# First convolution of an attention-and-convolution kernel: image pairs with 2x4 output tiles in place of single images with row pairs, and a head's last sums divided anew among VectorE and ScalarE

## The chip, the cores and the metric

The kernel runs on one core of one Trainium2 chip. A core has TensorE (PE, matrix products into PSUM), VectorE (DVE), ScalarE (ACT), GpSimd (POOL), SyncE (SP, which only issues transfers here) and 16 DMA engines. The metric is the device time of one execution in microseconds; lower is better.

## What is computed

The input x has 16 images of 128 channels by 32 by 32 points. Layer 0 is self-attention with 4 heads of 128 channels over the 1024 points of an image, plus x. Layer 1 is two quantized 3x3 convolutions, each followed by a batch normalisation over all images, and again the layer's input is added.

```python
def layer0(x, w_qkv, b_qkv, w_out, b_out):        # einsums of 1x1 convolutions
    qkv = einsum('bchw,oc->bohw', x, w_qkv) + b_qkv
    ...
    attn = softmax(einsum('bnc,bcm->bnm', q, k) * c ** -0.5)
    out = einsum('bnm,bmc->bnc', attn, v)
    ...
    return einsum('bchw,oc->bohw', out, w_out) + b_out + x

def layer1(x, w1, w2, gamma1, beta1, gamma2, beta2):
    out = act_quant(x)                            # clip to 0..1, 15 levels
    out = batchnorm(conv3x3(out, weight_quant(w1)), gamma1, beta1)
    out = act_quant(out)
    out = batchnorm(conv3x3(out, weight_quant(w2)), gamma2, beta2)
    return out + x
```

The first normalisation needs the statistics of all 16 images of the first convolution, so the second convolution can begin only when the attention of the last image is done.

## The kernel before

Everything concerned lies in `fast_path`. Its first part goes over 64 heads (16 images of 4). A head has 4 steps, and there are 252 steps for all heads but the last, which has a loop of its own in smaller units. In a step `scores` (L543 on) makes four 128x512 tiles of scores on PE (`pss`), ScalarE turns each into exponentials (L551), and VectorE forms their sums and differences for a seven-product scheme: L554, then L555 over two tiles at once, then L558; from a head's second step on L562 or L564 also adds to the running softmax sums `es`. The exponentials of a step are in one of two buffers `e`. `attend` then makes the seven products of the step before (`psa`), the second of which needs what L558 writes. So PE's order is: scores of step s, attention of step s-1, scores of step s+1. Each product of 128 output channels is issued as two halves of 64 columns of the PE array (`halves`, L410 on; the profile shows all products made through helpers as line L403).

Other work is hung on this sequence by a table: `at(step, half, fn, ...)` puts a function behind the scores (half 0) or behind the attention (half 1) of a step, and `run` calls what stands there. All table times are written by hand. Each engine's order is fixed when the program is built; it follows these calls, but not exactly (in the trace a piece of `transform_rows` stands between L555 and L558).

At a head's end (`end` is the first step of the next head) `sum_up` reduces `es` to quadrants (L625) in (end, 0). `evacuate` and three parts of `combine` take the four `psa` banks to SBUF with ScalarE and add them on VectorE, at end, end+1 and end+2. `normalise` at (end+2, 1) calls `inverse_sums`, which moves four 32x32 blocks to the first partitions (L652), sums them, takes the reciprocal (L654 to L658), copies it to the other three quadrants (L660) and spreads it (L664), all on VectorE; then it multiplies and adds to the image's accumulator (L673 to L679).

After an image's fourth head its first convolution is made while the next image's attention runs. `quantize` at (end+3, 0) writes a bf16 image with a border into one of three `pads`. `transform_rows` (L782, at (end+4, 0)) forms four row combinations of 16x34 elements, a scheme that gives two output rows at a time. `rows_product` (at end+6 to end+8) makes four products of three taps each, in halves: 24 matmuls of 512 columns per image into the one PSUM buffer of `ps_m` (`psw`), each copied out by ScalarE (L798). `rows_output` (L805, L806, L808) forms the rows on VectorE, and `first_statistics` takes the normalisation's statistics. `ps_m` is shared with the projections `psu` (steps 1 and 2 of a head) and `psv` (eight half steps of an image's third and fourth head). Images 9 to 14 (`AWAY`) send their convolution result to HBM (`y1d`); the second part reads it back in one transfer (L987). The last image has its convolution after the last head.

Of the kernel before, what the change touches and what calls it, by code (L numbers as in the profile page):

```python
# [9 lines left out]
F32 = mybir.dt.float32  # L10
# [4 lines left out]
PSUM = bass.MemoryType.PSUM  # L15

NH = 4
A_LEVELS = 15.0
W_LEVELS = 7.0
BN_EPS = 1e-5  # L20
# [171 lines left out]
def fast_path(  # L192
# [44 lines left out]
    for n in range(2):  # L237
        nc.gpsimd.memset(late[n][:, 0:1], float((B - 1) * N))

    AWAY = range(9, B - 1)  # L240
    ys = [None if b in AWAY else keep.tile([P, N], F32, name=f"y{b}") for b in range(B)]
    pads = []
    for i in range(NPAD):
        t = padp.tile([P, H + 2, W + 2], BF16, name=f"pad{i}")
# [128 lines left out]
    with ExitStack() as ph:  # L373
# [257 lines left out]
            )  # L631
            return part

        def sum_up(g):
            sides[g] = quadrant_sums(sides[g].rearrange("p a n -> p (a n)"))

        def inverse_sums(g, part, cut):

            n = (cut.stop - cut.start) // Q
            rinv = sums[:, g, cut.start // Q : cut.stop // Q]  # L640
            if g == LAST:

                ps = ps_m.tile([P, n], F32, tag="mm", name=f"psr_{g}_{cut.start}")
                w = part.shape[1] // n
                for i in range(w):
                    product(ps, quad, part[:, ts(i, n)], start=(i == 0), stop=(i == w - 1))
                nc.vector.reciprocal(rinv, ps)
            else:

                side = smp.tile([Q, P // Q, n], F32, tag="side", name=f"side_{g}")  # L650
                for a in range(P // Q):
                    nc.vector.tensor_copy(side[:, a, :], part[ts(a, Q), :])  # L652
                total = smp.tile([Q, n], F32, tag="total", name=f"total_{g}")
                nc.vector.tensor_reduce(total, side.rearrange("p a k -> p k a"), AX.X, ALU.add)  # L654

                first, second = total[:, 0 : n // 2], total[:, n // 2 :]
                nc.vector.tensor_tensor(first, first, second, ALU.add)
                nc.vector.reciprocal(rinv[0:Q, :], total)  # L658
                for a in range(1, P // Q):
                    nc.vector.tensor_copy(rinv[ts(a, Q), :], rinv[0:Q, :])  # L660


            rb = rbp.tile([P, N], F32, tag="rb", name=f"rb_{g}")[:, cut]
            nc.vector.transpose(rb, rinv.unsqueeze(2).to_broadcast([P, n, Q]))  # L664
            return rb

        def normalise(g):
            b, h = heads[g]
            rb = inverse_sums(g, sides.pop(g), slice(0, N))
            av = avs.pop(g)  # L670
            if h == 0:
                accs[b] = accp.tile([P, N], F32, tag="acc", name=f"acc_{b}")
                nc.vector.tensor_tensor(accs[b], av, rb, ALU.mult)  # L673
                return
            nc.vector.tensor_tensor(av, av, rb, ALU.mult)  # L675
            nc.vector.tensor_tensor(accs[b], accs[b], av, ALU.add)
            if h == NH - 1 or g == LAST - 1:

                nc.vector.scalar_tensor_tensor(accs[b], accs[b], bo2_sb, xt[b], ALU.add, ALU.add)  # L679
            if h == NH - 1:  # L680
                nc.sync.dma_start(out=x1d[b], in_=accs[b])
# [25 lines left out]
        def attend_unit(u):  # L707
# [30 lines left out]
            if final:  # L738
                avs[LAST, i] = psa[LAST, i]
                sides[LAST, i] = quadrant_sums(total)  # L740
            elif u + 1 == FIRST_UNIT[i + 1]:
                if i == 0:
                    avs["last"] = stp.tile([P, N], F32, tag="y", name=f"y_{LAST}")
                avs[LAST, i] = avs["last"][:, slice(*GROUPS[i])]
                nc.scalar.copy(avs[LAST, i], psa[LAST, i])
                sides[LAST, i] = quadrant_sums(total)

        def normalise_group(i):
            b, h = heads[LAST]
            x1 = accs[b]  # L750
            cut = slice(*GROUPS[i])
            rb = inverse_sums(LAST, sides.pop((LAST, i)), cut)
            nc.vector.tensor_tensor(rb, avs.pop((LAST, i)), rb, ALU.mult)
            nc.vector.tensor_tensor(x1[:, cut], x1[:, cut], rb, ALU.add)
            done = quantize(b, x1, A_LEVELS, 0.0, cut.start // W, cut.stop // W)
            quantized[:] = [done.ins]
            if i == len(GROUPS) - 1:
                nc.sync.dma_start(out=x1d[b], in_=x1)
# [1 line left out]

        middle1 = once.tile([P, 2, 3, P], BF16, name="middle1")
        taps1 = wq[0].rearrange("p (y x) o -> p y x o", x=3)
        weights1 = (taps1[:, 0], middle1[:, 0], middle1[:, 1], taps1[:, 2])
        D = H // 2
        FOUR = ((0, 2, ALU.subtract), (1, 2, ALU.add), (2, 1, ALU.subtract), (1, 3, ALU.subtract))
        works, ms = {}, {}

        def transform_weights():  # L770
            with tc.issue_after(sums_added[0]):
                nc.vector.tensor_tensor(middle1[:, 1], taps1[:, 0], taps1[:, 2], ALU.add)
                nc.vector.tensor_tensor(middle1[:, 0], middle1[:, 1], taps1[:, 1], ALU.add)
                nc.vector.tensor_tensor(middle1[:, 1], middle1[:, 1], taps1[:, 1], ALU.subtract)

        def transform_rows(b):
            pad = pads[b % NPAD]
            works[b] = once.tile([P, 4, D, W + 2], BF16, tag="rows", name=f"rows_{b}")
            pick = lambda r: pad[:, r : r + 2 * D - 1 : 2, :]
            for k in (1, 2, 0, 3):  # L780
                x_, y_, op = FOUR[k]
                nc.vector.tensor_tensor(works[b][:, k], pick(x_), pick(y_), op)  # L782

        def rows_product(b, k):
            ps = ps_m.tile([P, D, W], F32, tag="mm", name=f"psw_{b}_{k}")
            for dx in range(3):
                halves(
                    ps,
                    lambda t: weights1[k][:, dx, LANES[t]],
                    works[b][:, k, :, dx : dx + W],  # L790
                    start=(dx == 0),
                    stop=(dx == 2),
                )
            inner = k in (1, 2)
            if k < 2:
                ms[b, inner] = qtp.tile([P, 2, D, W], F32, tag="qt", name=f"m_{b}_{k}")

            nc.scalar.mul(ms[b, inner][:, k // 2], ps, (1.0, 0.5, 0.5, -1.0)[k])  # L798

        def rows_output(b):  # L800
            inner, others = ms.pop((b, True)), ms.pop((b, False))
            if b in AWAY:
                ys[b] = stp.tile([P, N], F32, tag="y", name=f"y_{b}")
            both = once.tile([P, 2, D, W], F32, tag="tiles", name=f"both_{b}")
            nc.vector.tensor_tensor(both[:, 0], inner[:, 0], inner[:, 1], ALU.add)  # L805
            nc.vector.tensor_tensor(both[:, 1], inner[:, 0], inner[:, 1], ALU.subtract)  # L806
            y = ys[b].rearrange("p (i r w) -> p r i w", r=2, w=W)
            nc.vector.tensor_tensor(y, others, both, ALU.add)  # L808

        def first_statistics(b):  # L810
            statistics(b, 0)
            if b in AWAY:
                nc.sync.dma_start(out=y1d[b - AWAY.start], in_=ys[b])

        def first_conv(r, rows, group):

# [53 lines left out]
        for g in range(LAST):  # L870
            b, h = heads[g]

            end = (g + 1) * NK
            at(end, 0, sum_up, g)
            at(end, 1, evacuate, g)
            at(end + 1, 0, combine, g, 0)
            at(end + 1, 1, combine, g, 1)
            at(end + 2, 0, combine, g, 2)
            at(end + 2, 1, normalise, g)
            if g > 0:  # L880
                at(g * NK + 1, 0, project_u, g + 1, 0)
                at(g * NK + 2, 0, project_u, g + 1, 1)
            if h == NH - 1:
                at(end + 3, 0, lambda b: quantize(b, accs[b], A_LEVELS, 0.0), b)
                at(end + 3, 1, sums_range, b)
                at(end + 4, 0, transform_rows, b)
                for i, k in enumerate((1, 2, 0, 3)):
                    at(end + 6 + (i + 1) // 2, (i + 1) % 2, rows_product, b, k)
                at(end + 8, 1, rows_output, b)
                at(end + 9, 0, first_statistics, b)  # L890
                if b + 2 < B:
                    at(end + 5, 0, load, b + 2, nc.scalar)
            elif h == NH - 2 and b + 1 < B:

                when = ((4, 0), (4, 1), (6, 1), (7, 0), (7, 1), (8, 0), (8, 1), (9, 1))
                for i, (step, half) in enumerate(when):
                    at(g * NK + step, half, project_v, b + 1, *divmod(i, 2))
        at(2, 1, project_u, 1, 0)
        at(3, 1, project_u, 1, 1)
        at(n_steps, 1, gather, 0)  # L900

        for step in range(n_steps):
            g, k = divmod(step, NK)
# [289 lines left out]
def attention_then_quantized_convs(  # L1193
# [49 lines left out]
    def conv_weights(n, wp, behind):  # L1243
# [15 lines left out]
            wq[n].rearrange("p t o -> p (t o)"), raw, MAGIC, None, ALU.subtract  # L1259
        )  # L1260

        nc.vector.tensor_scalar(sc[n], alpha, 1.0 / (A_LEVELS * W_LEVELS), None, ALU.mult)

    flag = const.tile([1, 1], mybir.dt.int32, name="flag")
    fast_path(
# [84 lines left out]
```

## Time and profile before

| | |
|---|---|
| median of two runs | 2024.57 us (2023.04 to 2026.1) |
| the profiled execution, its own time | 2024.57 us |
| its span, first to last instruction | 2022.7 us |
| PE, DVE, ACT busy | 1987.6, 1722.2, 1198.5 us |
| first part, steps of heads | to about 1894 us |
| from there to the end | last head, second convolution, output |

Busy times are unions of the records of an engine. A record of VectorE usually ends a little after the next one has begun, so a group's sum of durations is larger than the time it occupies. PE's ends are modelled, and two halves of the array can be at work at once, so PE's rows are read by the starts of their instructions. In steady stretches two images take 238.8 us, always the same.

### The profile page before, as it was taken

Reading aid. Unit: us, or ns where it says so; the run is one execution under the profiler, and the core shown is the slowest. Engines: PE = TensorE matmul, PEld = TensorE weight load, DVE = VectorE, ACT = ScalarE, POOL = GpSimd, SP = SyncE. Lnnn points to the kernel's source line nnn. Section 1 sums busy time; section 2 is a strip of 40 time slices with the busy share of each in tenths; the row PEclk is TensorE's granted clock in tenths of the full one; section 3 lists DMA queues with packets and bytes.
Section 4 is the critical chain, followed back from the end, with each engine's and each line's share of the span. In section 5 each row is a group of like instructions: output and inputs, shape, how many; then the busy total and the mean of one; then the engine's idle time right before and its main releaser. Section 6 shows DMA issues by size and latency. Waiting matters only on the chain. (4 is left out here: it accounts for less than half of the span.)

```text
span 2022.7 us, 24701 instructions
## 1 busy us (share of the span) xinstructions
PE 1987.6 (98%) x9497; PEld 730.3 (36%) x9497; DVE 1722.2 (85%) x2642; ACT 1198.5 (59%) x2007; POOL 19.7 (1%) x29
## 2 busy tenths in 40 slices
PE   9999999999999999999999999999999999999994
PEld 3543333333333333333333333433333333333441
DVE  5889888888888888888888888888888888878888
ACT  4565665665566566566556556656656655655575
POOL 0000000000000000000000000000000000000020
PEclk9999999999999999999999999999999999999997
DMA  1000000000000000000000000000000000000064
GB/s 42 24 1 22 1 22 1 22 0 1 22 1 22 1 9 14 0 22 1 21 1 1 22 1 21 11 22 11 1 22 11 22 11 21 11 1 11 11 239 168
DMA packets 12846, 43.74 MB, mean 22 GB/s; under 512 B 1456, under 2 KB 1840, under 8 KB 12720
## 3 DMA queue, kind: packets, MB, share of 16 engines
q1 hardware_dynamic: 9520, 32.05, 4.2%
q10 hardware_dynamic: 3200, 10.03, 1.5%
q8 instruction: 76, 1.25, 0.3%
q14 instruction: 50, 0.41, 0.1%
HBM read 22.16 MB, written 19.92 MB: 21 GB/s over the span
## 5 line engine op out<-in xcount | busy, mean ns | idle before, releaser
L403 PE MATMUL pss<-u,x 128*64 128x512 f32 (+1 forms) x4128 | 1031.9, 589 | 1.6 <-ACT u L509 1.6
L403 PE MATMUL psa<-e,vo 128*64 128x512 f32 (+1 forms) x3624 | 922.4, 588 | 0.0
L551 ACT ACTIVATE e<-pss 128x512 f32<-128x512 f32 x1008 | 595.4, 596 | 380.7 <-PE pss L403 331.9
L403 PEld LDWEIGHTS pss<-u,x 128*64 128x64 f32 x4128 | 351.6, 137 | 549.3 <-issue 493.4
L403 PEld LDWEIGHTS psa<-e,vo 128*64 128x64 f32 x3624 | 304.8, 137 | 483.5 <-issue 449.6
L555 DVE TENSOR_TENSOR e<-e 128x1024 f32<-128x1024 f32 x252 | 307.7, 1221 | 29.8 <-ACT e L551 21.6
L554 DVE TENSOR_TENSOR e<-e 128x512 f32<-128x512 f32 x252 | 172.2, 683 | 105.5 <-ACT e L551 101.7
L558 DVE TENSOR_TENSOR e<-e 128x512 f32<-128x512 f32 x252 | 174.0, 690 | 21.5 <-DVE e L555 0.5
L595 ACT COPY ev<-psa 128x512 f32<-128x512 f32 x252 | 135.5, 589 | 87.2 <-PE psa L403 87.0
L403 PE MATMUL psu<-x,at_sb 128*64 128x512 f32 x512 | 184.9, 599 | 1.0 <-DMA x<-in_x_dram 1.0
L403 PE MATMUL psv<-bt_sb,x 128*64 128x512 f32 x512 | 184.9, 592 | 1.0 <-ACT bt_sb L480 1.0
L530 ACT COPY vo<-psv 128x512 f32<-128x512 f32 x128 | 75.5, 590 | 142.3 <-PE psv L403 142.3
L564 DVE TENSOR_TENSOR es<-es,e 128x1024 f32<-128x1024 f32 x126 | 154.0, 1222 | 2.7
L509 ACT ACTIVATE u<-psu,au_sb 128x512 f32<-128x512 f32 x127 | 87.4, 688 | 21.7 <-PE psu L403 20.1
L798 ACT ACTIVATE m<-psw 128x512 f32<-128x512 f32 x60 | 35.9, 598 | 92.6 <-PE psw L403 90.7
L608 DVE TENSOR_TENSOR y<-ev,y 128x512 f32<-128x512 f32 x63 | 43.6, 692 | 52.4 <-ACT y L606 52.4
L664 DVE STREAM_TRANSPOSE rb<-sums 128x1024 f32<-128x1024 f32 (+1 forms) x66 | 79.8, 1210 | 1.6
L625 DVE TRANSPOSE_TENSOR_REDUCE part<-es 128x32 f32<-128x1024 f32 (+1 forms) x65 | 79.6, 1224 | 1.1
L403 PEld LDWEIGHTS psv<-bt_sb,x 128*64 128x64 f32 x512 | 53.6, 137 | 73.5 <-issue 66.7
L403 PEld LDWEIGHTS psu<-x,at_sb 128*64 128x64 f32 x512 | 53.5, 138 | 73.1 <-issue 69.1
L562 DVE TENSOR_TENSOR es<-e,e 128x1024 f32<-128x1024 f32 x63 | 76.8, 1219 | 0.0
L675 DVE TENSOR_TENSOR av<-av,rb 128x1024 f32<-128x1024 f32 x47 | 57.6, 1225 | 1.6
(159 smaller groups left out, 1193.6 us busy)
## 6 DMA issues: line engine op xcount, KB each, us to landing
x_dram<-acc SPq DMA_DIRECT2D x16, 512.0 KB, 4.3
x<-in_x_dram ACTq DMA_DIRECT2D x15, 512.0 KB, 4.6
res<-x_dram SPq DMA_DIRECT2D x1, 7680.0 KB, 30.0
y_dram<-y SPq DMA_DIRECT2D x6, 512.0 KB, 2.6
back<-y_dram SPq DMA_DIRECT2D x1, 3072.0 KB, 11.4
out_dram<-back SPq DMA_DIRECT2D x6, 512.0 KB, 4.5
out_dram<-y SPq DMA_DIRECT2D x5, 512.0 KB, 4.1
out_dram<-y SPq DMA_DIRECT2D x9, 256.0 KB, 2.5
```

The costliest lines, as they stand in the source:

```text
L403: done = nc.tensor.matmul(out_, lhsT=lhsT, rhs=rhs, start=start, stop=stop)
L509: copied = nc.scalar.activation(dst, ps, AF.Identity, bias=au_sb[:, h : h + 1])
L530: nc.scalar.copy(v[:, c : c + 3 : 2], ps.rearrange("p (h a o) -> p a h o", a=2, o=PH))
L551: exps[:] = [nc.scalar.activation(e[:, 2 * c + 1 - m], ps, AF.Exp).ins]
L554: nc.vector.tensor_tensor(e[:, T3], e[:, B12], e[:, B22], ALU.add)
L555: nc.vector.tensor_tensor(e[:, T1 : T2 + 1 : T2 - T1], e[:, B12 : B11 + 1], e[:, B11 : T3 + 1 : T3 - B11], ALU.subtract)
L558: nc.vector.tensor_tensor(e[:, T4], e[:, T2], e[:, B21], ALU.add)
L562: nc.vector.tensor_tensor(sides[g], es[g, 0][:, T4 : T3 + 1], mine, ALU.add)
L564: added = nc.vector.tensor_tensor(sides[g], sides[g], mine, ALU.add)
L595: nc.scalar.copy(to, ps)
L625: nc.vector.tensor_reduce(part, total.rearrange("p (k c) -> p k c", c=Q), AX.X, ALU.add, apply_transpose=True,)
L664: nc.vector.transpose(rb, rinv.unsqueeze(2).to_broadcast([P, n, Q]))
```

## The change

1. Images are taken in pairs (0 and 1, up to 12 and 13). Along columns four outputs are formed from six input combinations, along rows two outputs from four: 24 products of 256 columns for two images, each in halves, so 48 matmuls of 256 columns per pair, where there were 48 of 512.
2. VectorE forms the combinations: `six_columns` in three stages s = 0, 1, 2 (28 operations of 34x8 elements per pair, which read every fourth bf16 column of `pads`), `six_rows` (24 operations of 2x16x8 elements), and, when ScalarE has copied four products out, the sums in `six_products` (three operations of 512, 256 and 256 elements for each of six columns, and ten of 512 elements per pair that read or write every fourth f32 column of the result `y2`).
3. Image 14 stands alone, with four outputs from 16 products of 256 columns (`transform_columns`, `products`).
4. The weights' transform is larger (some 18 operations, once). The weights and the scale get a factor 24 that cancels.
5. A head's seven 32x32 copies go to ScalarE, `inverse_sums` is cut into `sum_up` parts 1 to 3, and a head's end takes a step more: `combine` parts 1 and 2 at end+2 and end+3, `normalise` at (end+3, 1); quantizing follows at (end+5, 0). The last head of the step loop keeps a shorter plan.
6. Images 6 to 13 send their result away, two per transfer of 1 MB; `y1d` holds eight.

The diff, cut to its core:

```diff
-    AWAY = range(9, B - 1)
+    AWAY = range(6, B - 2)
...
+            elif part == 1:
                 side = smp.tile([Q, P // Q, n], F32, tag="side", name=f"side_{g}")
                 for a in range(P // Q):
-                    nc.vector.tensor_copy(side[:, a, :], part[ts(a, Q), :])
+                    nc.scalar.copy(side[:, a, :], sides[g][ts(a, Q), :])
...
                 for a in range(1, P // Q):
-                    nc.vector.tensor_copy(rinv[ts(a, Q), :], rinv[0:Q, :])
+                    nc.scalar.copy(rinv[ts(a, Q), :], rinv[0:Q, :])
...
+        def six_columns(p, s, g):
+            if g == 0:
+                works[p] = once.tile([P, 8, ROWS, D4], BF16, tag="rows", name=f"work_{p}_{s}")
+            pad = pads[(2 * p + g) % NPAD]
+            at = lambda c: pad[:, :, c : c + 4 * D4 - 3 : 4]
+            one, two = works[p][:, g], works[p][:, 2 + g]
+            t, u = works[p][:, 4 + g], works[p][:, 6 + g]
+            if s == 0:
+                nc.vector.tensor_tensor(t, at(1), at(2), add)
+                nc.vector.tensor_tensor(u, at(3), at(4), add)
+                nc.vector.scalar_tensor_tensor(one, t, -4.0, u, mult, add)
...
+        def six_rows(p, s, i):
+            if i == 0:
+                tiles[p] = once.tile(
                    [P, 2, 4, 2 * D * D4], BF16, tag="tiles", name=f"tiles_{p}_{s}"
                )
+            pick = lambda r: works[p][:, 2 * i : 2 * i + 2, r : r + 2 * D - 1 : 2, :]
+            for k, (x, y, op) in enumerate(OF_FOUR):
+                into = tiles[p][:, i, k].rearrange("p (g i j) -> p g i j", g=2, j=D4)
+                nc.vector.tensor_tensor(into, pick(x), pick(y), op)
...
+        def two_products(name, weights, operands, scale, k):
+            if k == 0:
+                ms[name] = qtp.tile([P, 4, 2 * P], F32, tag="qt", name=f"wino_{name}")
+            ps = ps_m.tile([P, 2, 2 * P], F32, tag="mm", name=f"psw_{name}_{k}")
+            for i in range(2):
+                halves(ps[:, i], lambda t: weights[:, k + i, LANES[t]], operands(k + i))
+            nc.scalar.mul(ms[name][:, k : k + 2], ps, scale)
+            return ms[name]
...
+            nc.vector.tensor_tensor(e, two, of(2).unsqueeze(1).to_broadcast(list(two.shape)), ALU.add)
+            nc.vector.tensor_tensor(e[:, 0], e[:, 0], of(3), ALU.add)
+            nc.vector.tensor_tensor(e[:, 1], e[:, 1], of(3), ALU.subtract)
...
+            elif i == 1:
+                sums, differences = (y[0], y[1]) if s == 0 else (y[2], y[3])
+                nc.vector.tensor_tensor(sums, one, other, ALU.add)
+                nc.vector.tensor_tensor(differences, one, other, ALU.subtract)
+                if s == 1:
+                    nc.vector.tensor_tensor(y[0], y[0], y[2], ALU.add)
+                    nc.vector.scalar_tensor_tensor(y[2], y[2], 3.0, y[0], ALU.mult, ALU.add)
+                    nc.vector.scalar_tensor_tensor(y[1], y[3], 2.0, y[1], ALU.mult, ALU.add)
+                    nc.vector.scalar_tensor_tensor(y[3], y[3], 6.0, y[1], ALU.mult, ALU.add)
...
-            at(end + 1, 1, combine, g, 1)
-            at(end + 2, 0, combine, g, 2)
-            at(end + 2, 1, normalise, g)
+            at(end + 1, int(g < LAST - 1), sum_up, g, 1)
+
+            if g < LAST - 1:
+                at(end + 2, 0, combine, g, 1)
+                at(end + 2, 0, sum_up, g, 2)
+                at(end + 3, 0, combine, g, 2)
+                at(end + 3, 0, sum_up, g, 3)
+                at(end + 3, 1, normalise, g)
...
+                elif b % 2 == 1:
+                    p = b // 2
+                    columns = ((5, 1), (6, 0)), ((8, 0), (8, 1)), ((12, 0), (12, 1))
+                    rows_ = ((6, 1), (7, 0)), ((10, 0), (10, 1)), ((19, 0), (19, 1))
+                    when = ((7, 1), (8, 0), (8, 1), (9, 1)), ((11, 0), (11, 1), (13, 1), (18, 1))
+                    when += (((20, 1), (21, 1), (22, 1), (23, 0)),)
...
+                    at(end + 24, 0, first_statistics, b)
```

## The prediction

> **What bounds the kernel now.** I read the page's busy line and slices first.
>
> ```profile
> PE 1987.6 (98%) x9497; PEld 730.3 (36%) x9497; DVE 1722.2 (85%) x2642; ACT 1198.5 (59%) x2007; POOL 19.7 (1%) x29
> ...
> PE   9999999999999999999999999999999999999994
> ...
> DVE  5889888888888888888888888888888888878888
> ```
>
> PE is full to the last slice. The table of windows shows it head by head, for the four heads of one image (the next image repeats them):
>
> ```profile
> 735.00:765.00 30.00, 30.00 (x142) 10.17 (x140) 26.19 (x42) 18.56 (x31) 0.00 (x0) 1.00 0.10 36
> 765.00:794.50 29.50, 29.50 (x148) 11.06 (x146) 25.02 (x36) 17.65 (x30) 0.00 (x0) 1.00 0.00 1
> 794.50:822.60 28.10, 28.10 (x136) 9.99 (x134) 25.32 (x37) 16.46 (x28) 0.00 (x0) 1.00 0.00 1
> 822.60:854.40 31.80, 31.80 (x150) 10.80 (x148) 26.03 (x42) 18.57 (x33) 0.00 (x0) 1.00 0.00 1
> ...
> sum 238.80, PE 238.80 PEld 84.06 DVE 205.11 ACT 142.48 POOL 0.00; mean PE 29.85 PEld 10.51 DVE 25.64 ACT 17.81 POOL 0.00
> ```
>
> After each length stand PE, PEld, DVE and ACT. PE never stops: the steady part is PE's, and each microsecond taken from PE there is one of time, as long as VectorE keeps up. It has 33.7 us left in 238.8. How late it may be, the timeline shows at the step that starts at 765.05:
>
> ```profile
> 772.50 0.69 DVE L558 TENSOR_TENSOR e<-e 128x512 f32<-128x512 f32 x1
> ...
> 774.25 3.17 PE L403 MATMUL psa<-e,vo 128*64 128x512 f32 x13
> ...
> 777.68 1.22 DVE L562 TENSOR_TENSOR es<-e,e 128x1024 f32<-128x1024 f32 x1
> ...
> 778.99 1.20 ACT L551 ACTIVATE e<-pss 128x512 f32<-128x512 f32 x2 [0.58 <-DVE es L562]
> ```
>
> L558 ends at 773.19, 5.0 us after the step's last exponential (768.18), and its attention starts at 774.25: 1.1 us to spare. In the next step it ends at 776.60, 0.9 us after the last exponential, for an attention at 781.54: 4.9 us. So VectorE may fall some 5 us behind, and the old kernel uses 4 of them after an image's end. A second limit: exponentials of a head's third step wait for L562, since `e` has two buffers (46.9 us of such waits in all, hidden so far by three score banks).
>
> The groups give the sizes:
>
> ```profile
> L403 PE MATMUL psw<-rows,wq 128*64 128x512 bf16 x180 | 37.8, 383 | 0.0
> L403 PE MATMUL psw<-rows,middle 128*64 128x512 bf16 x180 | 37.4, 383 | 0.0
> L282 PE MATMUL psc<-pad,wq 128*128 128x256 bf16 x45 | 5.5, 274 | 0.3 <-DVE pad L1007 0.3
> ...
> L652 DVE COPY side<-part 32x32 f32<-32x32 f32 x252 | 42.9, 170 | 4.6
> L660 DVE COPY sums<-sums 32x32 f32<-32x32 f32 x189 | 32.6, 173 | 3.8
> L782 DVE TENSOR_TENSOR rows<-pad 128x544 bf16<-128x544 bf16 x60 | 24.9, 436 | 0.5
> L654 DVE TENSOR_REDUCE total<-side 32x32 f32<-32x128 f32 x63 | 23.0, 366 | 2.2
> ```
>
> The psw rows overstate PE's cost. In the timeline six of them begin at 1023.30 and regular scores go on at 1024.38; two halves for 1.08 us, less 0.43 each for a psa and a pss within, leave 1.30, so 0.216 us of one half for each: both halves work at once, and 24 cost 24 x 0.108 = 2.6 us per image.
>
> **What the Trainium skill says.** "VectorE: DVE Perf Modes", perf-mode tier table and the errata section: f32 tensor_tensor takes (N+151)/0.96 ns, bf16 goes double only at step 1. The trace agrees: 691 ns for 512 f32 (685 here), (272+151)/0.96 = 441 for the 544 bf16 of L782 (436). "TensorE: Matmul & The Clock Gate", back-to-back issue gap: N/2.4 + 2.5, so 109 ns for 256 columns; the trace has 5.5/45 = 122 at full width. "ScalarE: Activation LUTs", What ACT_TABLE_LOAD costs: 186 + 0.833 N, 93 of it overlapped; 612 for 512 columns, trace 617. "SBUF — State Buffer", Door 1, the note on cachelines: each access to a new 16-byte line pays; f32 at step 4 is just that. No size is given; L654, 128 elements at a wide step, takes 366 where the range's reductions of 128 in a row (L348, L349) take 245 and 278, so up to 0.9 ns an element.
>
> **PE, part by part.** Removed per pair: 48 x 0.108 = 5.2 us. Added: 48 products of 256, per half 24 x 0.109 to 0.122 = 2.6 to 2.9. Saved 2.5 us per pair, 17.3 for seven. Weight loads are 110 ns for bf16 beside 107 of columns; if they don't hide, all is lost, if they do, nothing more comes. Image 14: 2.6 - 16 x 0.11 = 0.8. Sum -18.1.
>
> **VectorE.** An independent successor starts some 0.08 us before a record ends (544 bf16 occupy 0.35 us, 512 f32 0.60, 1024 f32 1.14, by the starts in the timeline). Removed per pair: 56 small copies, 8 x (0.72 + 0.55) = 10.2; row transforms 8 x 0.35 = 2.8; outputs 2 x (0.60 + 0.60 + 1.14) = 4.7: 17.7. Added: six_columns 28 x (0.44 - 0.08) = 10.1; six_rows, 256 elements at double rate, 24 x (0.29 - 0.08) = 5.0, at single rate 8.2; the sums of a column 6 x (0.60 + 2 x 0.34) = 7.7; ten operations on y2 6.0; chained ones wait for each other, 0 to 3, I take 1.5; strided f32 0 to 10 x 512 x 0.9 ns = 4.6, I take 2, since half are writes. Together 32.3, bounds 28.8 and 39.6. Net +14.6 (11 to 22): 219.7 of PE's 236.3 us. It fits on average, not by place. By heads from the pair's end on, VectorE | PE:
>
> head 1 23.3 | 30.0; head 2 29.9 | 27.8; head 3 30.1 | 28.6; head 4 27.6 | 32.0; head 5 29.9 | 30.2; head 6 27.7 | 28.4; head 7 22.9 | 27.5; head 8 24.7 | 31.8.
>
> These are the windows above less 1.3 for the copies, with quantizing (1.7) moved on one head, the old image work out, and the stages where the table puts them: head 2 has s = 0 (twelve column operations 4.3, eight row ones 1.7), head 3 three sums of a column, two of y2, s = 1 and its rows (9.6), head 5 the large output at step 18 and eight row operations at step 19 (6.6). The 3.5 us for chains and strides come on top, mostly in heads 3 and 5.
>
> Heads 2 and 3 ask 60.0 + 1.4 of 56.4 us: 5 us behind, and on top of that the wave within a head (combine and normalise, 4.6 us, now all in its fourth step beside 6.4 us of PE), of which the old kernel's 1.1 us of margin shows the size. Of 5 to 6 us that may be late, 2 to 3 are missing. In head 5, step 18 asks 3.9 for L554 to L564, 1.5 for combine and the sum's chain, 1.3 and 3.6 for sums and result, step 19 asks 3.9, 1.2 for combine, 3.4 + 1.2 for normalise after a fourth head, 1.7 for rows: 22, and 2 for chains and strides, beside PE's 14; the lag starts near zero: again 2 to 3 missing. What is late then is L558 for the attention, and L562, which holds the exponentials of a third step. I take 5 us of new PE stall per pair; bounds 0 (the fixed order puts sums first and the wave doesn't add) and 11.5 (all added work at the upper price).
>
> **The rest.** ScalarE gets 56 x 0.12 to 0.21 us and four more copies of products (2.4): 142.5 becomes about 154 of 236, costs nothing while no copy waits; a copy that waits for a late VectorE sum has exponentials queued behind it, but each now stands a step after its source. ps_m's products are a half step (3 us) from any other use and need 0.6 to be copied. Transfers of y1d: one of 1 MB for two of 512 KB on SP, 17 steps before the buffer is needed: nothing. The read back grows from 3 MB in 11.4 us to 4 MB, about 15.2: issued at 1928.3, there at 1943.5; image 7, now the first in it, is quantized at 1943.7: 0 to 1, I take 0.5. Weights' transform: some 5 us more VectorE once, at 87 busy in 100: 0 to 5, I take 1. Image 14: about 15 us for 4 on VectorE in the last eight steps: 0 to 4, I take 1.
>
> **Sum.** -18.1 + 0.5 + 1 + 1 = -15.6, stalls 7 x 5 = +35: +19.4. Span 2022.7 + 19.4 = 2042.1; 1.9 us lie around it (the execution's own 2024.57 is also the median): 2044.
>
> **Rivals.** (a) The lag is hidden: PE's gain stays, 2009. For it: 16 us still free per pair, order by readiness; against: 60 of 56 in heads 2 and 3. Chance 0.24. (b) Slower by over 2%, VectorE as the bound, by one mechanism: short rows and strides cost more than the plain price. Rows of eight at single rate (3.2) and y2 at the full stride (2.6) give 5.8 us more per pair, in the full heads: 2044 + 7 x 5.8 = 2085. It decides from 8 us of stall per pair, 3 more than I take. For it the L654 row, against it that L782's rows of 34 run double. Chance 0.25. (c) 256 columns don't cost less, weight loads bind: +17 on PE, 3 us less stall per pair: about 2040. Against it 122 ns above, with weights twice as wide. Chance 0.05. My forecast, 2025 to 2065: 0.46.
>
> **How the numbers follow.** 2% is about what a measurement of this kernel can tell from no change: 1984 and 2065. Faster by that would need 40 us, more than PE's 18: 0.02. Slower 0.25, same 0.73. The range goes from (a) with small change, 2007, to (b), 2088; the likeliest's own is 2025 to 2065.
>
> **What would show it.** The psw products: 24 per half at 0.11 us. Steady pairs of 238.8 less 2.5 plus stall; PE below full in head 3 and in steps 18 to 20 after a pair; PE loads waiting for L558's like, ACT for L562's. VectorE near 220 per pair. Wrong if PE stays full (a), if six_columns or y2 rows are far over 0.44 and 0.69 us (b), or if stalls stand elsewhere.

## The result, and the profile after

The changed kernel takes 2095.18 us (two runs, 2093.64 to 2096.73) where the one before takes 2024.57: a ratio of 1.0349, 95% interval 1.0302 to 1.0396. It is slower, by 70.6 us; the prediction said 2044, at most 2088. The span of its profiled execution is 2094.9 us, against 2022.7. Its line numbers are five higher for the attention (scores' exponentials L556, sums L559, L560, L563, running sum L567 or L569), and the products that L403 showed stand in L408.

The page's busy line and slices of PE and VectorE:

```profile
PE 2014.9 (96%) x9505; PEld 890.8 (43%) x9505; DVE 1796.4 (86%) x2692; ACT 1278.9 (61%) x2480; POOL 19.6 (1%) x29
...
PE   8999999999999999999999999999999999999994
...
DVE  4878788897988988898888988989789888889998
```

The slices hide it: PE still shows nine tenths, but a tenth of 52 us is five. The table of windows, one pair cut at the starts of its heads (after each length PE, PEld, DVE and ACT; later the granted clock), shows where PE stands still:

```profile
787.51:818.65 31.14, 29.52 (x139) 13.69 (x135) 27.14 (x44) 18.19 (x39) 0.00 (x0) 1.00 0.00 1
...
910.05:944.07 34.02, 30.76 (x145) 11.57 (x143) 31.29 (x47) 20.04 (x39) 0.00 (x0) 0.95 0.00 1
...
sum 247.24, PE 241.87 PEld 106.54 DVE 215.25 ACT 152.57 POOL 0.00; mean PE 30.23 PEld 13.32 DVE 26.91 ACT 19.07 POOL 0.00
```

A pair takes 247.0 to 247.7 us where it took 238.8. Cut at the starts of PE's scores, six steady pairs are 52 us longer together, the first pair 4, the last 28 steps 15, the part after them 1: the 72 us of the span. Within a pair it is heads 2 and 6, counted from the pair's end, that are longest over their old length, and there PE has gaps of 1.6 and 3.3 us.

The groups, kept apart by form, with the lines that the prediction priced:

```profile
L408 PE MATMUL psw<-tiles,wino 128*64 128x256 bf16 x368 | 64.2, 274 | 0.0
...
L649 ACT COPY side<-part 32x32 f32<-32x32 f32 x252 | 54.5, 216 | 179.1 <-DVE part L630 176.6
L853 DVE TENSOR_TENSOR tiles<-work 128x256 bf16<-128x256 bf16 x168 | 43.6, 283 | 0.0
...
L899 DVE TENSOR_TENSOR y<-six 128x512 f32<-128x512 f32 x14 | 16.1, 1151 | 0.0
L895 DVE TENSOR_TENSOR y<-y,six 128x512 f32<-128x512 f32 x14 | 15.8, 1129 | 0.0
...
L901 DVE TENSOR_TENSOR y<-y 128x512 f32<-128x512 f32 x7 | 7.8, 1120 | 0.0
```

The 274 ns of the psw row are not PE's price, since neighbours overlap. The starts in the timeline are:

```profile
901.86 0.27 PE L408 MATMUL psw<-tiles,wino 128*64 128x256 bf16 x1
...
901.97 0.27 PE L408 MATMUL psw<-tiles,wino 128*64 128x256 bf16 x1
...
902.08 0.59 PE L408 MATMUL pss<-u,x 128*64 128x512 f32 x1
...
902.29 0.38 PE L408 MATMUL psw<-tiles,wino 128*64 128x256 bf16 x2
...
902.51 3.17 PE L408 MATMUL pss<-u,x 128*64 128x512 f32 x14
```

Two products hold one half of the array from 901.86 to 902.08, two the other half from 902.29 to 902.51: 0.11 us each, as predicted.

Two things stand out. The sums that write `y2` take 1.12 to 1.15 us, where 512 f32 in a row take 0.69. And the small copies `side`, which were moved to ScalarE, wait 176.6 us there for VectorE's `part`. One such wait in the timeline, at the start of head 2 (a step's four exponentials are L556; in brackets the idle time before and what ended it):

```profile
787.51 0.60 ACT L556 ACTIVATE e<-pss 128x512 f32<-128x512 f32 x1 [3.31 <-PE pss L408]
...
788.80 1.25 DVE L630 TRANSPOSE_TENSOR_REDUCE part<-es 128x32 f32<-128x1024 f32 x1
...
790.08 0.90 ACT L649 COPY side<-part 32x32 f32<-32x32 f32 x4 [1.97 <-DVE part L630]
790.89 1.54 ACT L556 ACTIVATE e<-pss 128x512 f32<-128x512 f32 x3
...
793.90 0.67 ACT L662 COPY sums<-sums 32x32 f32<-32x32 f32 x3 [1.48 <-DVE sums L659]
...
796.51 0.64 ACT L556 ACTIVATE e<-pss 128x512 f32<-128x512 f32 x1
...
797.21 1.08 PE L408 MATMUL pss<-u,x 128*64 128x512 f32 x4 [1.62 <-ACT e L556]
```

In the table of steps the `side` copies are due in the second half of step end+1. In ScalarE's queue they stand in step end itself, here between its first and its second exponential, in other heads ahead of the first or behind a later one. VectorE, late with its column operations, delivers `part` at 790.05; until then ScalarE is idle for 1.97 us with three exponentials behind it, whose scores PE completes one after the other up to 790.0 (its sixteen score matmuls run from 785.98). The `sums` copies, due in step end+3, stand as early as step end+1 and hold ScalarE for another 1.48 us; the next step's first exponential begins only at 796.51, and PE waits 1.62 us for it.

The second place is head 6, after the six results of a pair (L898 to L904, 906.40 to 912.46):

```profile
914.51 0.69 DVE L563 TENSOR_TENSOR e<-e 128x512 f32<-128x512 f32 x1
...
915.25 4.73 PE L408 MATMUL psa<-e,vo 128*64 128x512 f32 x13 [2.71 <-DVE e L563]
...
918.53 0.90 ACT L649 COPY side<-part 32x32 f32<-32x32 f32 x4 [5.35 <-DVE part L630]
```

Here PE itself waits 2.71 us for L563, which VectorE reaches late behind the six results, and ScalarE stands idle at the copies for 5.35 us. The 13 matmuls after the gap take 4.73 us where 13 take 3.17 elsewhere (before, at 774.25). The windows over it, and those over the same place of a later pair, show why:

```profile
911.51:914.92 3.41, 1.03 (x5) 0.14 (x1) 3.41 (x6) 1.19 (x2) 0.00 (x0) 1.00 0.00 0
914.92:918.34 3.42, 3.09 (x8) 1.00 (x10) 3.42 (x6) 0.00 (x0) 0.00 (x0) 0.50 0.00 0
...
1652.21:1655.62 3.41, 2.52 (x11) 0.59 (x7) 3.41 (x6) 2.39 (x4) 0.00 (x0) 1.00 0.00 0
1655.62:1659.03 3.41, 1.60 (x8) 0.63 (x10) 3.41 (x7) 0.00 (x0) 0.00 (x0) 1.00 0.00 0
1659.03:1662.45 3.42, 3.42 (x22) 1.43 (x19) 3.42 (x5) 1.71 (x6) 0.00 (x0) 1.00 0.00 0
```

The granted clock is 0.50 from 914.92 on, for 3.4 us. "TensorE: Matmul & The Clock Gate" of the Trainium skill, Part 1, tells of such half clock, after an idle window of about 3.4 us. Here less was enough, and the length of the gap alone does not decide: the six steady pairs all have a gap of 2.7 to 3.0 us at this place, five have half clock after it, and the one of the last three lines has not (its gap is 2.70 us).

The half-clock stretches of one run stand on a grid of 3.413 us: the first six of this kernel start 73, 72, 73, 72 and 145 such units apart. Laid on that grid, the windows at full clock of all traces of this case, between 100 and 1900 us, show a rule. After each of the 27 in which PE (by its modelled ends) stood still for 1.94 us or more, the next window is at half clock; it is after none of the 134 with 0.9 to 1.91 us. The gap of 2.70 us lies across a border of the grid and counts as 0.9 and 1.8.

The pair with that gap takes 247.0 us, the five others 247.2 to 247.7. So half clock adds some 0.2 to 0.7 us to a pair, less than the 1.6 us by which it stretches the 13 products, and the rest of the stall is there without it.

### The profile page after: what moved, and what is told of

The parts are those of the page before. It is cut to its first block, busy times and chain, and to the rows that moved or that the text cites. A ratio compares the mean times of both kernels' runs of the same rounds, so it can differ in the third digit from the quotient of the medians.

```text
span 2094.9 us, 25194 instructions
## 1 busy us (share of the span) xinstructions
PE 2014.9 (96%) x9505; PEld 890.8 (43%) x9505; DVE 1796.4 (86%) x2692; ACT 1278.9 (61%) x2480; POOL 19.6 (1%) x29
## 4 chain that ended last, share of the span: by engine, by line
PE 64%; DVE 24%; ACT 8%; issue 3%; DMA 0%; POOL 0%; DVEq 0%; ACTq 0%
PE pss L408 27%; PE psa L408 26%; DVE e L560 4%; PE psv L408 4%; PE psu L408 4%; ACT e L556 3%; DVE es L569 2%; DVE e L563 2%; ACT ev L600 2%; DVE part L630 2%; DVE e L559 1%; DVE es L567 1%; PE psc L287 1%; ACT side L649 1%; DVE av L690 1%
## 5 line engine op out<-in xcount | busy, mean ns | idle before, releaser
L408 PE MATMUL pss<-u,x 128*64 128x512 f32 (+1 forms) x4128 | 1061.0, 592 | 25.8 <-ACT e L556 23.2
L408 PE MATMUL psa<-e,vo 128*64 128x512 f32 (+1 forms) x3624 | 934.6, 595 | 19.3 <-DVE e L563 19.3
L556 ACT ACTIVATE e<-pss 128x512 f32<-128x512 f32 x1008 | 579.9, 594 | 308.3 <-PE pss L408 258.6
L408 PEld LDWEIGHTS pss<-u,x 128*64 128x64 f32 x4128 | 405.5, 137 | 500.6 <-issue 343.1
L408 PEld LDWEIGHTS psa<-e,vo 128*64 128x64 f32 x3624 | 363.4, 138 | 463.7 <-issue 375.0
L560 DVE TENSOR_TENSOR e<-e 128x1024 f32<-128x1024 f32 x252 | 307.2, 1219 | 26.3 <-ACT e L556 23.7
L559 DVE TENSOR_TENSOR e<-e 128x512 f32<-128x512 f32 x252 | 172.2, 683 | 86.0 <-ACT e L556 85.3
L563 DVE TENSOR_TENSOR e<-e 128x512 f32<-128x512 f32 x252 | 172.4, 684 | 10.1 <-DVE e L560 0.9
L408 PE MATMUL psv<-bt_sb,x 128*64 128x512 f32 x512 | 179.7, 593 | 1.0 <-ACT bt_sb L485 1.0
L408 PE MATMUL psu<-x,at_sb 128*64 128x512 f32 x512 | 174.7, 604 | 2.3 <-ACT wino L862 1.5
L649 ACT COPY side<-part 32x32 f32<-32x32 f32 x252 | 54.5, 216 | 179.1 <-DVE part L630 176.6
L569 DVE TENSOR_TENSOR es<-es,e 128x1024 f32<-128x1024 f32 x126 | 153.8, 1220 | 1.9
L862 ACT ACTIVATE wino<-psw 128x512 f32<-128x512 f32 x92 | 55.0, 598 | 70.5 <-PE psw L408 69.3
L679 DVE STREAM_TRANSPOSE rb<-sums 128x1024 f32<-128x1024 f32 (+1 forms) x66 | 79.6, 1207 | 12.0 <-ACT sums L662 11.9
L613 DVE TENSOR_TENSOR y<-ev,y 128x512 f32<-128x512 f32 x63 | 43.3, 688 | 52.8 <-ACT y L611 52.8
L408 PEld LDWEIGHTS psv<-bt_sb,x 128*64 128x64 f32 x512 | 58.7, 137 | 61.3 <-issue 49.2
L408 PEld LDWEIGHTS psu<-x,at_sb 128*64 128x64 f32 x512 | 54.4, 139 | 65.8 <-issue 52.4
L567 DVE TENSOR_TENSOR es<-e,e 128x1024 f32<-128x1024 f32 x63 | 76.8, 1219 | 0.3
## 6 DMA issues: line engine op xcount, KB each, us to landing
back<-y_dram SPq DMA_DIRECT2D x1, 4096.0 KB, 14.1
```

The lines of the kernel that those rows point to most:

```text
L408: done = nc.tensor.matmul(out_, lhsT=lhsT, rhs=rhs, start=start, stop=stop)
L556: exps[:] = [nc.scalar.activation(e[:, 2 * c + 1 - m], ps, AF.Exp).ins]
L559: nc.vector.tensor_tensor(e[:, T3], e[:, B12], e[:, B22], ALU.add)
L560: nc.vector.tensor_tensor(e[:, T1 : T2 + 1 : T2 - T1], e[:, B12 : B11 + 1], e[:, B11 : T3 + 1 : T3 - B11], ALU.subtract)
L563: nc.vector.tensor_tensor(e[:, T4], e[:, T2], e[:, B21], ALU.add)
L567: nc.vector.tensor_tensor(sides[g], es[g, 0][:, T4 : T3 + 1], mine, ALU.add)
```

## The experiments

Two theories were on the table after this. **Q**: the order of ScalarE's queue loses the time, since copies that VectorE feeds stand ahead of exponentials. **V**: VectorE's load loses it, by place, the slow sums on `y2` above all, and the queue only shows it. All times below are medians, read against the kernel before on the same chip (2023.8 to 2025.2 us); losses and gains are differences from it.

**1. Undo the small copies' move.** The changed kernel, with the seven copies of a head back on VectorE.

```diff
-                    nc.scalar.copy(side[:, a, :], sides[g][ts(a, Q), :])
+                    nc.vector.tensor_copy(side[:, a, :], sides[g][ts(a, Q), :])
...
-                    nc.scalar.copy(rinv[ts(a, Q), :], rinv[0:Q, :])
+                    nc.vector.tensor_copy(rinv[ts(a, Q), :], rinv[0:Q, :])
```

> The changed kernel with the seven 32x32 copies of a head on VectorE again, all else kept. Theory Q (ScalarE's queue: the side copies stand ahead of a head's first exponentials and wait for VectorE's part): the stalls at steps 4 and 12 after a pair and part of those at step 20 go, some 6 us per pair, so about 2050 us. Theory V (VectorE has too much work, the strided result above all): VectorE gets 10 us more per pair, so slower than the changed kernel's 2095, 2110 or more.

Measured: 2099.8 us (2097.85 to 2100.28), ratio 1.0366 (1.0349 to 1.0383). Q's 2050 is missed by far, and so is V's 2110: the 4 us over the changed kernel lie within the two intervals. The waits only moved: two copies in `combine`, which were on ScalarE before the change too and read VectorE's sums (L617 and L620), now hold the exponentials.

```profile
ACT ev L620 <- DVE y L618: 57.9, 39, 2.2
...
ACT ev L617 <- DVE y L613: 24.8, 24, 1.6
```

**2. Take the stride out of the results.** The changed kernel, with the four outputs of a row as four planes of `y2` instead of every fourth column. What is left out: the second convolution doesn't put the planes together again and reads points at wrong places.

```diff
-                y2[p].rearrange("p g (i j c) -> p (g i) j c", j=D4, c=4)[..., c] for c in range(4)
+                y2[p][:, :, ts(c, N // 4)] for c in range(4)
```

> The changed kernel with the pair's result kept in four planes of 256 elements in a row, so that the ten operations on it have no step of 16 bytes. The points of an image then lie in another order, and the second convolution reads them at wrong places. Both theories: these operations take 0.69 us and not 1.12. Q: only the stall at step 20 shrinks, 2 to 3 us per pair, so 2070 to 2080. V: most stalls go, 2020 to 2035.

Measured: 2071.8 us, ratio 1.0228 (1.0211 to 1.0246). The sums fall to the plain price:

```profile
L898 DVE TENSOR_TENSOR y<-six 128x512 f32<-128x512 f32 x14 | 9.5, 682 | 0.0
...
L901 DVE TENSOR_TENSOR y<-y 128x512 f32<-128x512 f32 x7 | 4.8, 682 | 0.0
```

VectorE has 3.7 us less work per pair (215.2 to 211.5), and 24 us of the loss go: 3 us per pair, and some at the end. Step 20, from its first exponential to the next step's, falls from 11.9 to 9.30 us; step 4, the first of head 2, stays at 8.98. Q's range held, V's 2020 to 2035 did not: a third of the loss hangs on the stride.

**3. Tie the small copies behind an exponential.** Nothing computed is changed; only the place of the copies in ScalarE's queue.

```diff
+                    with tc.issue_after(exps[0]):
-                    nc.scalar.copy(side[:, a, :], sides[g][ts(a, Q), :])
+                        nc.scalar.copy(side[:, a, :], sides[g][ts(a, Q), :])
```

and the same for `sums`.

> The changed kernel with the ScalarE copies tied behind the last exponential of the step that the table names (end+1 and end+3), all else kept. Q: the exponentials of a head's first step wait no longer for VectorE, some 6 us less stall per pair, about 2050. V: nothing changes, 2090 to 2100.

Measured: 2083.0 us, ratio 1.029 (1.0268 to 1.0312), between the numbers of the two theories. The waits of `side` are gone, and once more `combine`'s copies take their place (L620 for L618 67.0 us, L617 for L613 22.4). So the queue has four such groups of copies, and tying two of them leaves the other two in the way.

**4. The new head's end alone.** The kernel before with part 5 of the change and its old convolution, set one to two and a half steps later.

> The kernel before, with the first convolution of single images, and the new head's end alone: the copies on ScalarE, a step more for combine and normalise, the image's quantizing and products a step or two later. Q: the copies stand ahead of exponentials here too, so slower than before, 2030 to 2060. V: VectorE has 10 us less per two images, so as fast as before, 2015 to 2026.

Measured: 2080.8 us (2078.7 to 2081.5), ratio 1.0272 (1.0255 to 1.0289), worse than both theories said. VectorE has 193.7 us of work per pair, 11 less than before, and a pair takes 246.1 us. The waits and the timeline of this kernel (its lines are those of before from L551 on, with `part` L625, `side` L644):

```profile
ACT side L644 <- DVE part L625: 256.8, 63, 5.6
```

```profile
787.01 0.22 ACT L644 COPY side<-part 32x32 f32<-32x32 f32 x1 [5.40 <-DVE part L625]
787.13 0.58 ACT L551 ACTIVATE e<-pss 128x512 f32<-128x512 f32 x1
...
787.77 1.08 PE L403 MATMUL pss<-u,x 128*64 128x512 f32 x4 [1.22 <-ACT e L551]
```

Every head has the wait (63 times), with 5.4 us of idle ScalarE and 1.2 us of idle PE at this one. The length of such a wait is not its price: ScalarE waits here in the kernel before too, 3.3 us for the scores (at 765.05), and all 256.8 us of waits cost 56. A load theory can't explain it: VectorE has less to do than in the kernel before.

**5. The new head's end alone, tied.** The same, with all four groups of copies that VectorE feeds (`side`, `sums` and the two in `combine`) tied as in 3.

> The kernel before with the new head's end alone, and the four copies tied behind exponentials. Q: the loss of the new head's end (56 us untied) goes for the most part, 2020 to 2035. V, or a cost of the longer head's end itself: it stays at 2070 to 2085.

Measured: 2027.0 us (20 runs), ratio 1.0018 (1.0011 to 1.0025). A pair is 238.8 us again, PE full. The waits list of `side` on `part` has no entry any more, and what is left beside it is

```profile
DVE total L651 <- ACT side L647: 7.0, 16, 0.5
```

on VectorE, which loses nothing by it. The 52 us between 4 and 5 (55.6 and 3.2 over the kernel before) are the order of one queue, at nearly the same load of VectorE (193.7 and 191.7 us per pair). With the right order ScalarE's copies are indeed free, as the prediction had them.

**6. The whole change, tied.** The changed kernel with the same four ties.

> The changed kernel with all four ScalarE copies of a head's end that read what VectorE has just written (side, sums, and the two of combine) tied behind the last exponential of the step that the table names. Theory Q (ScalarE's order: such copies stand ahead of exponentials and wait): of 9 us stall per pair left with two of them tied, 4 to 6 more go: 2040 to 2055. Theory V (VectorE's load alone): no change against the two tied, 2080 to 2090.

Measured: 2067.3 us (2064.3 to 2071.4), ratio 1.0213 (1.0195 to 1.0231), a pair 242.6 us. Both theories' numbers are missed; 27 us of the change's 71 go with the order alone. Step 4 shows it best: 6.48 us before, 8.98 in the change and in experiment 2, and 6.49 here. The rest stands in steps 20 and 21, where PE waits for VectorE.

**7. The whole change, tied, and planes.** Experiments 2 and 6 together (the second convolution again reads points at wrong places).

> As pinned_all, and the pair's result in four planes, so that the strided operations go (the second convolution reads points at wrong places). Q: the two gains add, with most of PE's saving left, 2010 to 2030. V: as the planes alone, 2070.

Measured: 2035.4 us (2032.9 to 2037.1), ratio 1.0052 (1.0036 to 1.0069), a pair 238.9: 5 us above Q's range, far from V's 2070. Once the order is mended, the stride is worth 32 us, more than alone. One stall is left, in step 21 (10.1 us), and the timeline there shows VectorE without a gap and the exponentials behind it:

```profile
898.12 0.68 DVE L563 TENSOR_TENSOR e<-e 128x512 f32<-128x512 f32 x1
...
899.33 1.21 DVE L567 TENSOR_TENSOR es<-e,e 128x1024 f32<-128x1024 f32 x1
...
900.63 1.57 ACT L556 ACTIVATE e<-pss 128x512 f32<-128x512 f32 x3 [3.06 <-DVE es L567]
...
901.28 1.08 PE L408 MATMUL pss<-u,x 128*64 128x512 f32 x4 [1.94 <-ACT e L556]
```

This is the prediction's second limit, the two `e` buffers: L567 frees one.

**8. The convolution alone.** The changed kernel with the head's end of before.

> The new convolution of pairs alone, with the head's end of before (small copies on VectorE, combine and normalise a step earlier). Q: without side copies on ScalarE's queue the stalls are those of VectorE's load and of combine's copies, 8 us per pair, 2060 to 2080. V: 10 us more VectorE work per pair than in the changed kernel, slower than it, 2100 to 2130.

Measured: 2100.1 us, ratio 1.037 (1.0353 to 1.0388). Q's range is missed, V's just reached, though the kernel is not clearly slower than the changed one. It is experiment 1 again, within the intervals, with the same 225.7 us on VectorE per pair and the same waits, so the extra step in a head's end does nothing by itself that shows here. The two parts of the change don't add: head's end alone +56, convolution alone +76, both +71.

**9 and 10. The convolution alone, its two copies in `combine` tied; and with planes.** These ask which of queue and load rules when the small copies stay on VectorE.

> The convolution change with the head's end of before (2100.1 us), and the two copies of combine that read VectorE's sums tied behind the exponentials of their half. If the order of ScalarE's queue is the larger part of the loss here as it was in the head's end alone, 2045 to 2070 us and a pair of 240 to 243.5 us, with the waits of these two copies no longer ahead of exponentials. If VectorE's load of 225.7 us per pair is the larger part, the run stays at 2080 to 2100 us.

> The same with the outputs as four planes (the second convolution then reads points at wrong places). VectorE has some 5 us less per pair. Queue and slow sums together as the whole loss: 2025 to 2045 us. If the head's end of before, whose small copies stay on VectorE (about 10 us per pair), is itself too much load: 2050 to 2075 us.

Measured: 2092.1 us, ratio 1.034 (1.0311 to 1.037), and 2057.1, ratio 1.0159 (1.0142 to 1.0176). Here tying gives 8 us, hardly more than the noise (the four executions of 9 go from 2086.7 to 2099.3), and the stride 35. In 9 the exponentials wait for L567 instead:

```profile
ACT e L556 <- DVE es L567: 88.1, 39, 3.3
```

With 225 us of VectorE work per pair V is the larger part, as its ranges for both runs said, and the move of the small copies off VectorE, with the longer head's end, is worth 25 us (2092.1 to 2067.3, experiment 6), provided that they are tied.

**11. The last third of a pair's work three steps later.** Experiment 7 with the row sums at steps (22,1) and (23,0), the products from (23,1) on and the statistics at 27, for all pairs but the last; and with the second convolution reading the planes in their own order.

```diff
+                    if b < B - 3:
+                        rows_ = rows_[:2] + (((22, 1), (23, 0)),)
+                        when = when[:2] + (((23, 1), (24, 1), (25, 1), (26, 0)),)
...
+            y = ys[b].rearrange("p (c i j) -> p c i j", c=4, j=W // 4)[:, :, r0:r1]
+            t = t.rearrange("p (i j c) -> p c i j", j=W // 4, c=4)
```

> The changed kernel with the four copies tied and the outputs as four planes (2035.4 us), the second convolution now reading the planes in their own order, and the last third of a pair's work moved three steps on, out of the steps in which VectorE also normalises and quantises the next image. If the one stall left, in step 21, is VectorE's pile-up there, that step falls from 10.1 to under 8 us, a pair to 236.3 to 237.5 us, and the run to 2018 to 2027 us: only here would the 2.5 us per pair of saved PE time appear. If the pile-up is the head's end alone, or only moves three steps on, the pair stays at 238 to 239 us and the run at 2032 to 2038 us.

Measured: 2058.1 us, ratio 1.0175 (1.0158 to 1.0192): worse than 7 by 23, and outside both ranges. Step 21 falls only to 9.07 us, and step 26, where the products' sums now meet a head's end, rises from 7.23 to 9.07; a pair takes 240.3. Of the 20.0 us by which its span is longer than that of 7, 6 lie before the last step and 14 after it, most of them in reading the planes back into rows: the eight operations below take 8 x 1.42 = 11.4 us more. Of the quantizing step there, the tile `steps`, first this kernel and then experiment 7 (minimum, median and maximum in ns):

```profile
L1187 ACT ACTIVATE steps<-back,bias,scale x8: 2622/2660/2676, 1967.0 to 1994.3; 128x1024 bf16<-128x1024 f32 x8
```

```profile
L1180 ACT ACTIVATE steps<-back,bias,scale x8: 1227/1238/1248, 1953.6 to 1975.8; 128x1024 bf16<-128x1024 f32 x8
```

So the planes of experiments 2, 7, 10 and 12 flatter the change by up to about 14 us; that is what a whole version would pay in this form.

**12. Less on VectorE.** Experiment 7 with a part of VectorE's work left out: the four last sums of s = 1, and the column sums and result sums of s = 2. All products and their copies stay.

> The changed kernel with the four copies tied and the outputs as four planes (2035.4 us), and VectorE's work on the second half of the outputs left out: the four last sums of the second third, and the six column sums and two sums on the outputs of the last third. That is some 7 us of VectorE's 209.8 us per pair, around steps 18 to 23; the products and their copies stay. If the stall left in step 21 is VectorE's lateness, it goes, and the 2.5 us per pair by which the convolution's PE work is shorter shows for the first time: a pair of 236.2 to 237 us, the run at 2014 to 2022 us. If the products of 256 columns cost PE as much as those of before, or the stall has another cause, a pair stays at 238 to 239 us and the run at 2030 to 2037 us.

Measured: 2019.5 us (2018.24 to 2022.37), ratio 0.9975 (0.9964 to 0.9985), as expected for lateness. The windows over one pair, their sum line:

```profile
sum 237.09, PE 237.03 PEld 117.84 DVE 203.82 ACT 155.95 POOL 0.00; mean PE 29.63 PEld 14.73 DVE 25.48 ACT 19.49 POOL 0.00
```

PE is full at 237.1 us: the shorter products' gain shows, 1.7 us of the 2.5 predicted. Where the other 0.8 goes was not found. It takes a VectorE with 6 us less per pair to show it, so no complete version here beats the kernel before; the nearest complete version of the whole change is experiment 11.

## Why the prediction was wrong, step by step

- **PE bounds, and its saving.** Right in kind: with VectorE relieved, PE is full at 237.1 us per pair. The saving is 1.7 us, not 2.5; it was never to be had in the change as made. Rival (c) falls: a psw product takes 0.11 us of one half in the timeline of after.
- **VectorE's sum.** Predicted 219.7 us per pair, measured 215.2. Rows of eight bf16 run at double rate (L853, 256 elements in 0.283 us; 256 f32 take 0.420, L885), the column operations take 0.40 to 0.44. Rival (b), nearest in time with 2085, has only half its mechanism: its single rate isn't there, its stride is.
- **The stride.** The term "strided f32 0 to 10 x 512 x 0.9 ns = 4.6, I take 2, since half are writes" was mis-sized. The measured cost is 10 x 0.44 = 4.4 us, the upper bound, and a write alone pays it in full: L898 and L899 read in a row and take as long as L901, which also reads at the step. The Trainium skill's "SBUF — State Buffer", Door 1, names the kind of cost, and the runs give its size. It is worth 24 us in the change as made, and 32 with the order mended.
- **ScalarE's copies.** This is the step that failed: "costs nothing while no copy waits; a copy that waits for a late VectorE sum has exponentials queued behind it, but each now stands a step after its source". The danger was named and then put aside on the table's word. The table gives the step in which a piece of work is due, not its place in the queue, and in the queue `side` stands in the same step as its source. VectorE was late there, and 62 waits of 176.6 us together were the result. The prediction put this wait at nothing; in experiment 4 it alone costs 56 us, and 5 takes that to 3.2; in the whole change mending the order takes 27 (experiment 6).
- **The stall.** "I take 5 us of new PE stall per pair; bounds 0 ... and 11.5": about 11 per pair, worked out as 247.4 less the 236.3 that the prediction gave PE. The choice was wrong, since the queue was not in it. That 11 lies under the upper bound is luck: the bound stood for VectorE's work at the dearest price, and of the 11 us 4.7 go with the ties alone (experiment 6). Against the prediction's span (2042.1 for 2094.9, 53 us) the six steady pairs make 37 of the miss, the last 28 steps 12, and the first pair 4.
- **Where the stall stands.** Step 20 was named, steps 4 and 21 were not. Head 3, the other place named, hardly stalls (28.4 us for 28.1). The stall of head 2 is in its first step, since a wait in the queue needs no backlog over two heads.
- **The rest.** The read back takes 14.1 us for 15.2; the part after the last step is 1 us longer. The last eight steps were put at 1 us. The 15 us of the last 28 steps hold stalls of both kinds: from their first exponential to their last they are 14.3 us longer than before, 5.7 in experiment 7 and 0.6 in experiment 12, so image 14's own work is little.

What stays open: whether a plan of steps exists that keeps the whole convolution and still leaves PE full.

## What to carry to other kernels

A copy moved to a less busy engine is priced by what stands behind it in that engine's queue, not by its own 0.2 us: find its place there in the trace, ask which engine feeds it and how late that engine can be, and tie it behind the work that must not wait. Two causes that meet in one place don't add: here the load was worth 24 us before the order was mended and 32 after. When a bounding engine has gaps, a balance by heads is too coarse; the step in which two late things meet decides.

## What the runs showed of the hardware

- VectorE, 512 f32 with a step of 16 bytes on the written side: 1.12 us; with none, 0.68. Columns of bf16 read at a step of 8 bytes, 272 elements: 0.40 to 0.44 us. A scalar_tensor_tensor takes as long on 272 in a row (L832, 0.43); a tensor_tensor on 256 in rows of eight takes 0.28.
- ScalarE, 1024 elements from f32 to bf16, written at a step of 8 bytes: 2.66 us; in a row, 1.24.
- TensorE's clock, in these traces, is half for the next 3.41 us when PE stood still for 1.94 us or more of a 3.413 us window (27 windows of 27), and not at 1.91 us or less (none of 134); the windows lie on a fixed grid in each run. So a gap of 2.70 us that a border of the grid divides left it at full speed.
- A 32x32 copy takes 0.216 us on ScalarE and 0.170 on VectorE.
